# A graph attention layer on one core: the copy of a group's sums goes behind the next group's carried row, and the last two quads are weighted as one row of groups

## The chip, the cores and the metric

The kernel runs on one core of a Trainium2 chip. The core has five engines with instruction queues of their own: TensorE (PE, with its weight loads listed as PEld), VectorE (DVE), ScalarE (ACT), GpSimd (POOL) and SyncE (SP), which here issues the plain transfers. Each queue is worked off in order. The metric is the device time of one execution in microseconds, as the median over several runs. Times of single instructions come from one execution taken by the hardware profiler.

## The reference

12,500 nodes with 128 features each are joined by 200,000 edges, sorted by destination. Cut to what matters:

```python
h   = relu(layernorm(x));  hn = (h @ W_node.T).reshape(N, 4, 32)
e   = (edge_attr @ W_edge.T).reshape(E, 4, 32)
att = sum(concat([hn[src], hn[dst], e], -1) * a, -1);  att = where(att > 0, att, 0.2 * att)
m   = maximum(segment_max(att, dst), 0);  ex = exp(att - m[dst])
denom = segment_sum(ex, dst) + (E - deg)[:, None] * exp(-m)
out = x + segment_sum((ex / denom[dst])[..., None] * hn[src], dst)
```

So each destination needs the largest logit of its edges, a weighted sum of the gathered source rows, the sum of the weights and the number of its edges.

## The kernel before, in words

**Tiling.** The edges are cut into 392 groups of 511 (four chunks of 128, with one place left over), and four groups make a quad: 98 quads. Since the edges are sorted, a group's destinations lie in a window of 80 consecutive nodes. Quads are collected into supers of two to four quads (`supers`); the twenty in the middle have four. The logits of a super are brought into one softmax (`softmax`), while the groups of earlier quads are summed.

**Node stage.** At first the node rows are normalised and multiplied by the weights, and a table with 137 numbers a node is written to memory: the four heads' 32 values with a one each, a count and four logit parts.

**Gathers.** `gather` (L141) fetches 128 rows of the table for one chunk by an indirect transfer that POOL issues: 1494 from the table and 72 from `x` before the table is there. They run through a ring of eight quads, `ga`, and POOL issues them one behind the other.

**Logits.** `all_logits(q)` starts with `flush`, whose `add_sources` (L580) adds the source parts out of the gathered rows of the quad before it: it is the first instruction of a quad that needs that quad's gathers. Then, group by group, DVE compares destinations (L550) and PE multiplies (L556, L559).

**Sums.** `sums(q)` is a generator with one step for each group. A step weights the gathered rows (`weigh`, L766, 128x528 elements), makes the matrix that marks each edge's window place (L779), multiplies chunks 1 to 3 (L784), and then calls `complete()` for the group before it. The first place of chunk 0 is reserved for the *carried row*: row 96 of the sums of the group before that, scaled by DVE (L709) and with its count copied by ACT (L713), so that a destination whose edges run over a group's end is summed on. Then PE multiplies chunk 0 (L714), and ACT copies the 97x137 sums from PSUM to `pt` (L715). Three PSUM buffers named `acc` take the groups in turn. L709 and L715 of neighbouring groups read the same buffer, and DVE's instruction waits for ACT's.

**Division.** When a quad's last group is copied, ACT computes the exponentials of the denominator (L722), and `state["division"]` is left for the next `complete()`, where `divide` runs on DVE: L798, L801, L803, L807 (80x512), and L811, which adds `xw` to `res` (80x512; both in SBUF). SP then writes a row of windows for each group (L504), one in each step, each after the one before it because windows overlap. The last three quads are divided in parts, and three of the additions L811 are on POOL.

**Order.** All is under a manual schedule. `together` takes one step of each of its generators in turn: `sums` of one quad beside `all_logits` of another beside the stages of `softmax`. In the last super the flag is read that selects the slow path `tile_any_order`; it isn't taken for sorted edges.

**The two last quads.** For `q >= nq - 2` the window marks were made earlier on POOL (L741), and `weigh` runs one group ahead within its quad.

Of the kernel before, what the change touches and what calls it, by code (L numbers as in the profile page):

```python
# [16 lines left out]
H, HD = 4, 32  # L17
HW = HD + 1
# [6 lines left out]
R_CNT, R_SRC, ROW = H * HW, H * HW + 1, H * HW + 5  # L25
# [6 lines left out]
QG = 4  # L32
# [11 lines left out]
def blocks(total, step):  # L44
    return [(i, min(step, total - i)) for i in range(0, total, step)]
# [3 lines left out]
def kernel(  # L49
# [35 lines left out]
    nc = tc.nc  # L85
    NP = x.shape[0]
    G = dst_rows.shape[0]
# [34 lines left out]
    quads = blocks(G, QG)  # L122
    nq = len(quads)
# [6 lines left out]
    GA, GATHERED = {}, set()  # L130
# [26 lines left out]
    with tc.manual_schedule():  # L157
# [6 lines left out]
        for _ in range(AT_ONCE):  # L164
            q, i = early.pop(0)
# [301 lines left out]
    with tc.tile_pool(name="work", bufs=2) as work, \  # L467
# [13 lines left out]
        def groups(s):  # L481
            q0, m = supers[s]
            g0 = quads[q0][0]
            return g0, quads[q0 + m - 1][0] + quads[q0 + m - 1][1] - g0
# [30 lines left out]
        def fetch_inputs(q):  # L515
            g0, m = quads[q]
            xw = XW[q] = work.tile([SPAN, QG, D], F32, name="xw", bufs=4)
            at = ROWS[q] = windows(base_row, 4 * D, g0, m)
            due["inputs"] += [(as_bytes(xw[:, i, :]), rows_at(x, at[i], 4 * D)) for i in range(m)]
# [173 lines left out]
        begun = []  # L693
        state = {}

        def complete():

            division = None if "held" in state else state.pop("division", None)
            if begun:
                complete_group(*begun.pop())  # L700
            if division:
                divide(*division)

        def complete_group(q, i, ga, hot, pt, acc, fc):
            g0, m = quads[q]
            g = g0 + i
            if g:
                before = state["before"]
                nc.vector.tensor_tensor(  # L709
                    ga[0:1, i, 0, 0:H * HW].rearrange("p (h w) -> p h w", w=HW),  # L710
                    before[WIN:WIN + 1, 0:H * HW].rearrange("p (h w) -> p h w", w=HW),
                    fc.unsqueeze(2).to_broadcast([1, H, HW]), op=OP.mult)
                nc.scalar.copy(ga[0:1, i, 0, R_CNT:R_CNT + 1], before[WIN:WIN + 1, R_CNT:R_CNT + 1])  # L713
            nc.tensor.matmul(acc, hot[:, i, 0, :], ga[:, i, 0, :], start=False, stop=True)  # L714
            nc.scalar.copy(pt[:, i, :], acc)  # L715
            state["before"] = acc

            parts = {nq - 1: (2, 3), nq - 2: (2,), nq - 3: (2,)}.get(q, ())
            if i + 1 in parts or i == m - 1:
                lo = max([k for k in parts if k <= i], default=0)  # L720
                den = work.tile([SPAN, QG, H], F32, name="den")
                nc.scalar.activation(den[:, lo:i + 1, :], pt[0:SPAN, lo:i + 1, R_SRC:R_SRC + H],  # L722
                                     AF.Exp, scale=-1.0)
                state["division"] = q, pt, den, lo, i + 1


# [18 lines left out]
        def sums(q):  # L745

            for k in range(nq - 3, nq) if q == nq - 3 else [q] if q < nq - 3 else []:
                fetch_inputs(k)
            g0, m = quads[q]
            s = of_quad[q]  # L750
            s0, sm = groups(s)
            ga = GA.pop(q)
            heads = lambda t: t[:, :, 0:sm * H].rearrange("p j (h g) -> p j h g", h=H)
            ex, xs, facs = XS[s]
            fc = facs[WIN:WIN + 1, 0:sm * H].rearrange("p (h g) -> p h g", h=H)
            pt = work.tile([WIN + 1, QG, ROW], F32, name="pt", bufs=3)
            hot = HOT.pop(q) if q in HOT else marks(q)
            beside = xs[:, :, 0:sm * (H + 1)].rearrange("p j (h g) -> p g j h", g=sm)
            nc.scalar.copy(ga[:, :m, :, R_CNT:R_SRC + H], beside[:, g0 - s0:g0 - s0 + m])  # L759

            def weigh(i):

                if i < m:
                    val = ga[:, i, :, 0:H * HW].rearrange("p j (h w) -> p j h w", w=HW)
                    weight = heads(ex)[:, :, :, g0 + i - s0]
                    nc.vector.tensor_tensor(  # L766
                        val, val, weight.unsqueeze(3).to_broadcast([P, J, H, HW]), op=OP.mult)

            ahead = 1 if q >= nq - 2 else 0
            for i in range(ahead):  # L770
                weigh(i)
            for i in range(m):
                g = g0 + i
                if q == nq - 1 - FREE and i == 1:
                    for k in range(FREE):
                        HOT[nq - FREE + k] = marks(nq - FREE + k)
                weigh(i + ahead)
                if q < nq - FREE:
                    nc.vector.tensor_tensor(  # L779
                        hot[:, i, :, 0:SPAN], lane_ps.unsqueeze(1).to_broadcast([P, J, SPAN]),  # L780
                        slot[:, g, :].unsqueeze(2).to_broadcast([P, J, SPAN]), op=OP.is_equal)
                acc = ps.tile([P, 512], F32, name="acc", bufs=3)[0:WIN + 1, 0:ROW]
                for j in range(1, J):
                    nc.tensor.matmul(acc, hot[:, i, j, :], ga[:, i, j, :], start=j == 1, stop=False)  # L784
                complete()
                begun.append((q, i, ga, hot, pt, acc, fc[:, :, g - s0]))
                issue("inputs", "results", *(["inputs"] * 3 if q == nq - 3 else []))
                yield
# [90 lines left out]
        with tc.manual_schedule():  # L879
            for q in range(min(2, nq)):  # L880
                fetch(q)
                issue("weights", all_of=True)
            on_vector = nc.vector.tensor_copy
            assert supers[0] == (0, 2) and supers[1] == (2, 2)

            held = [(q, i) for q in range(raw, min(QUADS, nq)) for i in range(raws(q), quads[q][1])]
            GATHERED.update(range(raw, QUADS))

            def some(*numbers):
                for n in numbers:  # L890
                    for _ in range(min(n, len(held))):
                        held_gather(*held.pop(0), table, ROW)
                    yield

            together(some(2, 0, 1, 0, 1), *late(0, on_vector), normed(1))
            together(some(1, 0, 1, 0, 1), *late(1, on_vector), all_logits(0), normed(2))
            together(some(0, 0, 1), all_logits(1), raw_statistics(raw_pool, 3))
            check_steps = checked()
            for s, (q0, m) in enumerate(supers):


                ahead = list(range(q0 + m, sum(supers[s + 1]))) if s + 1 < len(supers) else []
                now, ahead = ahead[:1], ahead[1:]
                beside = [sums(q0 - 1)] if s not in (0, 2) else [] if s else late(2) + [raw_scaled(3)]
                beside += late(raw) if s == 1 else []
                turned_stage = softmax(s)
                if s == len(supers) - 1:

                    next(turned_stage)
                    redo = nc.values_load(flag[0:1, 0:1], min_val=0, max_val=1)  # L910
                    for _ in range(2):
                        next(beside[0])
                    state["held"] = True
                if not s:
                    beside.insert(0, some(1, 1, 1, 1, 1, len(held)))
                if s == len(supers) - 1:
                    together(turned_stage, *beside)
                else:
                    together(*beside, *map(all_logits, now), turned_stage)
                assert not held  # L920
                for k in range(m if s == 1 else m - 1):
                    now, ahead = ahead[:1], ahead[1:]
                    together(sums(q0 + k), *map(all_logits, now), *([] if s else [normed(raw)]))
                    if s > 4:
                        next(check_steps, None)
                if s == len(supers) - 2:
                    together(check_steps)
                if s < 2:
                    complete()
                for a in ahead:  # L930
                    together(all_logits(a))
                if not s:
                    together(*late(3))
            flush()
            last_sums = sums(nq - 1)
            together(last_sums)
            complete()
            complete()

    with tc.If(redo > 0):  # L940
# [195 lines left out]
```

## Time and profile before

| what | value |
|---|---|
| median of 3 runs | 2013.75 us (2011.76 to 2014.98) |
| the profiled execution: time, span | 2018.52 us, 2016.7 us |
| POOL busy | 1510.6 us, 75% of the span |
| DVE busy | 1323.2 us, 66% |
| PE busy | 1369.1 us, 68% |
| ACT busy | 406.3 us, 20% |
| mean granted TensorE clock | 0.539 |
| last gather issued | 1973.11 us to 1974.06 us |
| last DVE instruction ends | 2010.45 us |

A line of a group reads: source line, engine, operation, output and inputs with their shapes, count; then busy time and the mean of one in ns; then the idle time of the engine before them and what ended it. In the timeline a line reads: start and duration in us, engine, line, operation; the bracket is idle time before it and what ended it. In the list of waits: who waited for whom, the total in us, how often, the longest. POOL's busy share is below 100% because the time between two issues isn't counted as busy.

### The profile page before, as it was taken

The numbers are of one execution on the slowest core, as the hardware profiler recorded it, in microseconds if no ns is written. First come the engines' busy times: TensorE is split into PE (matmuls) and PEld (weight loads), VectorE is DVE, ScalarE is ACT, GpSimd is POOL, SyncE is SP. The second block draws the span as 40 slices with busy tenths as digits, with TensorE's granted clock in tenths as the row PEclk, the third lists the DMA queues.
The fourth block names the chain that finished last, engine by engine and source line by source line (L and its number), as shares of the span: only waits on it lengthen the run. The fifth ranks groups of instructions, "written<-read, shape, count | busy, mean of one in ns | idle before, by whom it ended". The sixth has DMA issues, their size and how long they took to land. (4 is left out here: it accounts for less than half of the span.)

```text
span 2016.7 us, 27090 instructions
## 1 busy us (share of the span) xinstructions
PE 1369.1 (68%) x7317; PEld 1243.8 (62%) x7317; DVE 1323.2 (66%) x3261; ACT 406.3 (20%) x1531; POOL 1510.6 (75%) x1609
## 2 busy tenths in 40 slices
PE   6577888766575757666757666666566666777776
PEld 5567788755565746555656566566565565766665
DVE  6676788666574766655656657556566475668776
ACT  6664122111111111111111111111111111112112
POOL 7777777777777777777777777777777777777774
PEclk8777555555555555555555555555555555555556
DMA  7654756544546455455545454545454545454531
GB/s 251 204 145 118 183 162 178 137 129 130 142 122 156 121 146 138 130 131 136 138 130 147 119 146 123 147 120 147 121 145 120 147 122 144 126 146 125 139 96 36
DMA packets 194091, 279.50 MB, mean 139 GB/s; under 512 B 79849, under 2 KB 143337, under 8 KB 186098
## 3 DMA queue, kind: packets, MB, share of 16 engines
q1 hardware_dynamic: 142128, 165.55, 30.0%
q0 software_dynamic: 50112, 109.61, 21.7%
q10 hardware_dynamic: 1698, 2.58, 0.4%
q8 instruction: 61, 1.00, 0.2%
q14 instruction: 92, 0.75, 0.1%
HBM read 254.25 MB, written 23.30 MB: 138 GB/s over the span
## 5 line engine op out<-in xcount | busy, mean ns | idle before, releaser
L141 POOL DMA_INDIRECT ga<-table,srci x1494 | 1422.9, 952 | 457.7 <-issue 384.0
L784 PE MATMUL acc<-ga,hot 128*97 128x137 f32 x2352 | 645.3, 446 | 54.1 <-ACT ga L759 25.4
L784 PEld LDWEIGHTS acc<-ga,hot 128*97 128x97 f32 x2352 | 516.8, 278 | 70.1 <-ACT ga L759 31.4
L556 PEld LDWEIGHTS <-at 80*128 80x128 bf16 x1568 | 211.0, 163 | 521.7 <-DVE at L550 504.4
L556 PE MATMUL lg<-pw,at 80*128 80x12 bf16 x1568 | 169.1, 181 | 445.8 <-DVE at L550 445.1
L559 PE MATMUL lg<-wblk,ea 128*128 128x8 f32 x1568 | 405.0, 356 | 0.0
L559 PEld LDWEIGHTS lg<-wblk,ea 128*128 128x128 f32 x1568 | 377.4, 306 | 0.0
L580 DVE TENSOR_TENSOR U<-st,ga 128x64 f32<-128x64 f32 x98 | 26.2, 268 | 436.1 <-DMA ga<-table,srci 428.8
L550 DVE TENSOR_TENSOR at<-const_ps,db 80x512 bf16<-80x512 f32 x392 | 267.3, 682 | 6.1
L766 DVE TENSOR_TENSOR ga<-ga,ex_ps 128x528 f32<-128x528 f32 x392 | 268.5, 685 | 0.6 <-issue 0.3
L714 PE MATMUL acc<-ga,hot 128*97 128x137 f32 x784 | 257.4, 431 | 2.8 <-ACT ga L713 2.7
L715 ACT COPY pt<-acc 97x137 f32<-97x137 f32 x392 | 107.4, 274 | 717.5 <-PE acc L714 715.1
L714 PEld LDWEIGHTS acc<-ga,hot 128*97 128x97 f32 x784 | 198.3, 282 | 4.9 <-ACT ga L713 4.6
L709 DVE TENSOR_TENSOR ga<-acc,facs 1x132 f32<-1x132 f32 x391 | 115.8, 296 | 121.8 <-ACT pt L715 111.9
L779 DVE TENSOR_TENSOR hot<-const_ps,slot 128x320 f32<-128x320 f32 x384 | 183.5, 478 | 0.0
L713 ACT COPY ga<-acc 1x1 f32<-1x1 f32 x391 | 59.9, 153 | 459.7 <-DVE ga L709 453.1
L141 POOL DMA_INDIRECT ga<-in_x_dram,srci x72 | 68.8, 955 | 23.1 <-issue 18.6
L807 DVE TENSOR_TENSOR res<-pt,const_ps 80x512 f32<-80x512 f32 (+2 forms) x102 | 67.5, 662 | 3.8 <-DVE const_ps L803 0.3
L811 DVE TENSOR_TENSOR res<-res,xw 80x512 f32<-80x512 f32 (+2 forms) x99 | 67.4, 681 | 3.4
L618 ACT ACTIVATE low<-t_ps 64x511 f32<-64x511 f32 (+2 forms) x28 | 16.5, 589 | 190.5 <-PE t_ps L616 190.5
L398 PE MATMUL row_ps<-wcat,hT 128*128 128x137 f32 x198 | 40.8, 358 | 20.7 <-DVE tgt L404 10.7
L568 DVE TENSOR_REDUCE st<-lg 128x64 f32<-128x192 f32 x98 | 35.0, 357 | 25.5 <-PE lg L559 24.6
(137 smaller groups left out, 1012.8 us busy)
## 6 DMA issues: line engine op xcount, KB each, us to landing
db<-in_dst_dram SPq DMA_DIRECT2D x98, 640.0 KB
ea<-in_edge_t_dram SPq DMA_DIRECT2D x98, 512.0 KB
ga<-table,srci POOLq DMA_INDIRECT x1494
xw<-in_x_dram SPq DMA_DIRECT2D x392, 40.0 KB
out_dram<-res SPq DMA_DIRECT2D x392, 40.0 KB
pw<-side SPq DMA_DIRECT2D x392, 1.9 KB
table<-row SPq DMA_DIRECT2D x9, 616.5 KB
xt<-in_x_dram SPq DMA_DIRECT2D x9, 576.0 KB
```

Of the source, the lines that this page charges most:

```text
L141: nc.gpsimd.indirect_dma_start(out=ga[:, i, j, 0:width], out_offset=None, in_=rows, in_offset=bass.IndirectOffsetOnAxis(ap=srci[:, g0 + i, ...
L550: nc.vector.tensor_tensor(at[:, i, :], node_ps[0:SPAN, g0 + i:g0 + i + 1].to_broadcast([SPAN, GE]), db[:, i, :], op=OP.is_equal)
L556: nc.tensor.matmul(lg[:, i, j].rearrange("p k h -> p (k h)"), at[:, i, j * P:(j + 1) * P], sw, start=i + j == 0, stop=False, skip_group_ch ...
L559: nc.tensor.matmul(lg[:, i, 2 * w:2 * w + 2, 0, :], ea[:, i, w, :], wblk, start=False, stop=True, skip_group_check=True)
L709: nc.vector.tensor_tensor(ga[0:1, i, 0, 0:H * HW].rearrange("p (h w) -> p h w", w=HW), before[WIN:WIN + 1, 0:H * HW].rearrange("p (h w) -> ...
L714: nc.tensor.matmul(acc, hot[:, i, 0, :], ga[:, i, 0, :], start=False, stop=True)
L715: nc.scalar.copy(pt[:, i, :], acc)
L766: nc.vector.tensor_tensor(val, val, weight.unsqueeze(3).to_broadcast([P, J, H, HW]), op=OP.mult)
L779: nc.vector.tensor_tensor(hot[:, i, :, 0:SPAN], lane_ps.unsqueeze(1).to_broadcast([P, J, SPAN]), slot[:, g, :].unsqueeze(2).to_broadcast([ ...
L784: nc.tensor.matmul(acc, hot[:, i, j, :], ga[:, i, j, :], start=j == 1, stop=False)
L807: nc.vector.tensor_tensor(res[:, :n, :].rearrange("p g (h d) -> p g h d", d=HD), val[:, :, :, 0:HD], share_ps[0:R, :n, :].unsqueeze(3).to_ ...
L811: add.tensor_tensor(res[:, :n, :], res[:, :n, :], xw, op=OP.add)
```

## The change

Four things are changed. `complete_group` is cut into `carry` (the carried row, and then the copy of the group *before*), `finish` (the last multiplication) and `copy_out` (copy, exponentials, leaving the division). So the copy of a group's sums stands on ACT behind the next group's L709 and L713 rather than ahead of them; since the division is left by the copy, it comes one step later. In the last two quads, a step calls `carry()` first, and weights a group ahead only then, and the two quads are one row: the last quad's first group is weighted in the last step of the quad before. Their two copies L759 are both made before that. A pending division is done at once where the last super begins, and the ends get another `complete()` and a `copy_out()`. The number of instructions of each kind is unchanged.

```diff
             if begun:
-                complete_group(*begun.pop())
+                carry()
+                finish(*begun.pop())
             if division:
                 divide(*division)
-        def complete_group(q, i, ga, hot, pt, acc, fc):
+        def carry():
+            if not begun or "carried" in state:
+                return
+            q, i, ga, hot, pt, acc, fc = begun[0]
+            state["carried"] = True
+            if quads[q][0] + i:
                 before = state["before"]
                 nc.vector.tensor_tensor(
...
                 nc.scalar.copy(ga[0:1, i, 0, R_CNT:R_CNT + 1], before[WIN:WIN + 1, R_CNT:R_CNT + 1])
+            copy_out()
+
+        def finish(q, i, ga, hot, pt, acc, fc):
+            del state["carried"]
             nc.tensor.matmul(acc, hot[:, i, 0, :], ga[:, i, 0, :], start=False, stop=True)
+            state["before"] = acc
+            state["uncopied"] = q, i, pt, acc
+
+        def copy_out():
+            if "uncopied" not in state:
+                return
+            q, i, pt, acc = state.pop("uncopied")
+            m = quads[q][1]
             nc.scalar.copy(pt[:, i, :], acc)
-            state["before"] = acc
...
-            ahead = 1 if q >= nq - 2 else 0
-            for i in range(ahead):
-                weigh(i)
+            if q == nq - 2:
+                weigh(g0)
             for i in range(m):
...
-                weigh(i + ahead)
+                if last_two:
+                    carry()
+                weigh(g + last_two)
...
+                    divide(*state.pop("division"))
                     state["held"] = True
...
                 if s < 2:
                     complete()
+                    copy_out()
...
             together(last_sums)
             complete()
+            complete()
+            copy_out()
             complete()
```

More of the change, by code (lines that the diff above doesn't have):

```diff
@@ L699, in complete @@
             if begun:
-                complete_group(*begun.pop())
+                carry()
+                finish(*begun.pop())
             if division:
                 divide(*division)
-        def complete_group(q, i, ga, hot, pt, acc, fc):
-            g0, m = quads[q]
-            g = g0 + i
-            if g:
+        def carry():
[4 more added lines that the diff above has]
+            if quads[q][0] + i:
                 before = state["before"]
@@ L723, in complete_group @@
                                      AF.Exp, scale=-1.0)
+                assert "division" not in state
                 state["division"] = q, pt, den, lo, i + 1
@@ L751, in sums @@
             s0, sm = groups(s)
-            ga = GA.pop(q)
+            ga = GA[q]
             heads = lambda t: t[:, :, 0:sm * H].rearrange("p j (h g) -> p j h g", h=H)
@@ L758, in sums, with weigh @@
             beside = xs[:, :, 0:sm * (H + 1)].rearrange("p j (h g) -> p g j h", g=sm)
[L759 to L765, printed above, removed]
+            last_two = q >= nq - 2
+            for k in (nq - 2, nq - 1) if q == nq - 2 else () if last_two else (q,):
+                lo, n = quads[k][0] - s0, quads[k][1]
+                nc.scalar.copy(GA[k][:, :n, :, R_CNT:R_SRC + H], beside[:, lo:lo + n])
+            def weigh(g):
+                k = g // QG
+                if g < G and (k == q or last_two):
+                    val = GA[k][:, g - k * QG, :, 0:H * HW].rearrange("p j (h w) -> p j h w", w=HW)
+                    weight = heads(ex)[:, :, :, g - s0]
                     nc.vector.tensor_tensor(
                         val, val, weight.unsqueeze(3).to_broadcast([P, J, H, HW]), op=OP.mult)
-            ahead = 1 if q >= nq - 2 else 0
-            for i in range(ahead):
-                weigh(i)
+            if q == nq - 2:
+                weigh(g0)
             for i in range(m):
```

## The prediction

> **What bounds the kernel now.** I read the page's groups first, then the list of waits, and then the timeline at one quad and at the end.
>
> ```profile
> L141 POOL DMA_INDIRECT ga<-table,srci x1494 | 1422.9, 952 | 457.7 <-issue 384.0
> L580 DVE TENSOR_TENSOR U<-st,ga 128x64 f32<-128x64 f32 x98 | 26.2, 268 | 436.1 <-DMA ga<-table,srci 428.8
> L709 DVE TENSOR_TENSOR ga<-acc,facs 1x132 f32<-1x132 f32 x391 | 115.8, 296 | 121.8 <-ACT pt L715 111.9
> ...
> L811 DVE TENSOR_TENSOR res<-res,xw 80x512 f32<-80x512 f32 (+2 forms) x99 | 67.4, 681 | 3.4
> ```
>
> ```profile
> POOL ga L141 <- issue: 402.6, 1320, 0.3
> ...
> DVE U L580 <- DMA ga<-table,srci: 428.8, 75, 11.9
> ...
> DVE ga L709 <- ACT pt L715: 111.9, 153, 2.2
> ```
>
> POOL issues a gather every 1.25 us (0.95 and 0.30) from the start to 1974.06 and, once the table is there, is never kept longer than 0.3. DVE waits for its rows at L580, 428.8 us in all. So POOL sets the pace up to 1974, and the 111.9 us that L709 waits for the copy lie, but for the last ones, inside DVE's larger wait. Shortening them is worth nothing there; only the end behind the last gather, or the length of a gather, can move the time.
>
> Gathers are not all equally long. The timeline, at a common quad and at another:
>
> ```profile
> 1011.81 0.95 POOL L141 DMA_INDIRECT ga<-table,srci  x1 [0.31 <-issue]
> 1011.93 0.27 DVE L580 TENSOR_TENSOR U<-st,ga 128x64 f32<-128x64 f32 x1 [5.68 <-DMA ga<-table,srci]
> ...
> 1013.79 0.30 DVE L709 TENSOR_TENSOR ga<-acc,facs 1x132 f32<-1x132 f32 x1
> ...
> 1015.57 0.94 POOL L141 DMA_INDIRECT ga<-table,srci  x1 [0.30 <-PE acc L784]
> 1015.58 0.71 DVE L811 TENSOR_TENSOR res<-res,xw 80x512 f32<-80x512 f32 x1
> 1016.00 0.28 ACT L715 COPY pt<-acc 97x137 f32<-97x137 f32 x1 [1.72 <-PE acc L714]
> ```
>
> ```profile
> 1336.28 0.69 DVE L811 TENSOR_TENSOR res<-res,xw 80x512 f32<-80x512 f32 x1
> 1336.37 1.42 POOL L141 DMA_INDIRECT ga<-table,srci  x1 [0.30 <-PE acc L784]
> ```
>
> Here L811 began 0.09 before the gather, and the gather took 1.42. Write d for L811's start less the gather's: d of -0.21 gave 1.30 (at 1763.02), -0.27 gave 1.24 (1158.26), -0.46 gave 1.05 (1078.10); d from 0.00 up gave 0.94 to 0.95. All fit one rule of this trace: the gather needs something at 0.13 us after its start, and waits until an L811 already running has ended: stretch = 0.56 + d, for d between -0.56 and about -0.03. L606, the only other long one of that kind, does the same (1.45 at 1374.35, d -0.04). Of the 10.6 us of stretch in this execution, 4.5 us fall on L811 (15 gathers) and 4.5 us on L606 (12). In the common quad L811 begins just as the gather does, and costs nothing.
>
> **The change part by part.**
>
> *Copy behind the carry, gathers still running.* ACT's L715 no longer stands before L709; per group DVE loses a wait of about 0.48 and ACT gets one. Worth nothing by itself: DVE waits at L580 for 5.7 to 8 us a quad. If that cover were gone it would be a gain, so it is costed at 0. PSUM buffers: a copy ends about 0.3 us behind L713, while L714 behind the same L713 takes 0.66, so PE finds its buffer free: 0.
>
> *The division moved by one step.* This moves L811 against the gathers' clock. Take the quad above. L709 at 13.79 stays. The next step now follows at once: L550 at +0.33, L766 +0.61, L779 +0.61, end of DVE's part +0.50, so 1015.84. L709 then waits for PE: L714 is done when ACT's copy began, 1016.00. L709 to L811 took 1.76 in unhindered quads (1315.04 to 1316.80). So L811 begins at 1017.77, and the gathers on the old clock at 1018.07 (1015.57 and two times 1.25): d = -0.30, stretch 0.26. This repeats: in 40 quads from 370 us on the copy stands 4.07 us behind L580, and L580 stands a fixed landing time behind a gather (mostly 0.05 to 0.16). Setting L811 at 4.07 + 1.76 behind each of these 40 L580s gives d from -0.57 to 0.50, most at -0.26 to -0.35, and stretches that add to 8.7 us. A stretched gather shifts all later ones and with them the next L580, so they add up.
>
> In quads with L606 (at 1293) the division's 2.04 no longer stand behind the first L709; L621 loses 0.15 of that to ACT's L618, so the second L709 comes at 1299.05 in place of 1300.94, L811 at 1300.81, the gather at 1301.34: d = -0.53, 0.03 each, for the 22 of them from 370 us on 0.7 us. In the 18 quads behind a softmax the same working gives 0.1 us. The old 4.5 us of L811 go; L606 keeps its place behind L580 and its 4.5. Net: 8.7 + 0.7 + 0.1 - 4.5 = +5.0 us. The unknown is d. If all 40 places are 0.15 earlier, the 40 cost 4.2; 0.2 later, 14.0; 0.3 later, 7.2 and falling. That makes the net between +0.5 and +10.3.
>
> The Trainium skill, GPSIMD Engine Reference, Key points, says that GpSimd shares its SBUF interfaces with VectorE, with contention from instructions with two SBUF inputs, and names no moment. By that alone L580 (0.12 behind a gather's start) or an L811 anywhere over a gather would cost too, before as after, and the change nothing; the trace has 0.94 to 0.95 us for these gathers, so the row decides.
>
> *SP's queue.* The output rows wait for L811 and so does what stands behind them: `pw`, `xw`, `ea` and `db` up to 2.2 us later. `pw` and `ea` are fetched two quads (40 us) ahead, `db` and `xw` about one (20 us): 0. POOL's queue keeps its order.
>
> *The end.* At the last super's start the division now stands behind carry, count, copy and exponential: L709 at 1974.19, then 0.30, 0.15, 0.28, 0.22 and 0.03 between each: L798 at 1975.23 in place of 1974.82, +0.41, and L580, L616 and the chain behind them. One division earlier leaves the way for L568, which waited for PE until 1970.18: PE then finds L550 0.75 sooner and loses 0.4 again a group later, -0.33. In the last two quads a link was L714, copy, L709, L713, L714: 1.36 (1997.33 to 1998.69); without the copy 1.05. But DVE fills it: by group 0.33 for L709, 0.61 for L766 and half of a division's 1.0, 1.45. Placing the rows in the new order, both L759 first, I get the first division of the last quad done at 2006.8 - 0.33 = 2006.5 in place of 2007.61. Behind it stand the four last output rows, 2007.64, 2009.14, 2011.87 and 2013.48: each waits for the one before, 1.5 to 2.7 us, so the end is theirs. Rows of the quads before hold some of it back: -0.6, between -1.3 (all of it) and +0.4 (nothing of the 0.33, and one more row of 2.7).
>
> Sum: +5.0 - 0.6 = +4.4 us. The profiled execution took 2018.52 (its span 2016.7 and 1.8 around it); it would take 2022.9. The median of the runs shown is 4.8 lower: 2013.75 + 4.4 = 2018.2.
>
> **The rivals.**
>
> *B, L811 misses the gathers.* If the second L709 begins 0.30 later, as it did before behind the copy, d is about 0.0 and no gather is stretched. Then only the old 4.5 us vanish: 2013.75 - 4.5 - 0.6 = 2008.7. It decides from 0.26 us later on. For it: landing times without the profiler aren't seen. Against: the copy's 4.07 is the same within 0.02 in nearly every such quad.
>
> *C, the gathers pay the same in all.* More L606 or L811 stretches without the profiler before, or fewer after, so that the sums cancel: the end alone, 2013.2. For it: 10 of the 40 L580s stand 0.3 to 1.2 behind a gather, so the landings do slip. The skill's rule taken without a moment gives this time too.
>
> *D, the end turns slower.* The granted clock in the last stage was 1.00 from 1995 to 2001, and 0.50 from 2002 to 2005. At 0.50 L784 repeats after 1.90 (1972.04 to 1973.94), longer than DVE's 1.45; with all at 0.50 the first division of the last quad comes 2.1 later: with the gathers as in C, 2015.3. The skill's TensorE: Matmul & The Clock Gate, part 1, grants full clock behind about 3.4 us of work; the 0.99 at 1988 to 1990, behind 3.8 us of unused multiplications, agrees.
>
> **How the numbers follow.** About 0.2%, 4.0 us, is what a measurement can tell from no change here. Forecast 0.66, of which 0.56 above 4.0 and 0.10 below (its d earlier by 0.1 or more); B 0.10, of which 0.07 faster and 0.03 within; C 0.18, within; D 0.06, of which 0.05 within and 0.01 above, on top of some stretch. Faster 0.07, within 0.36, slower 0.57. The range: up to +12.2 (the +10.3, +0.4 from the end and 1.5 for D), 2026; down to 2011, between B and C, which leaves out B and the forecast's far end. The forecast's own is 2013.7 (+0.5 - 0.6) to 2023.5 (+10.3 - 0.6).
>
> **What would show it.** Right: gathers of 1.15 to 1.3 us about once in each common quad, with an L811 begun 0.2 to 0.4 before them; L141's mean 4 to 6 ns higher; the last gather 5 us later against the first; L709 behind PE, never ACT; first division of the last quad about 1 us nearer to the last gather. Wrong: L811 at d above 0 or below -0.56 in the common quads, or stretched gathers without an L811; or an L709 that still waits 0.3 longer.

## The result, and the profile after

The changed kernel takes **2023.53 us** (median of 6 runs, 2020.85 to 2026.14), the kernel before 2014.37 (6 runs, 2011.76 to 2016.00). The ratio is 1.0044, with a 95% interval from 1.0033 to 1.0055: slower by 6.6 to 11.1 us, where 2018.2 us (+4.4) was forecast, with a range from 2011 to 2026. The kernel is slower, as forecast, but the 9.2 us between the medians are about twice the +4.4. The profiled execution of the changed kernel took 2026.14 us; its span is 2024.4, against 2016.7 before.

The groups of the changed kernel that answer to those shown of before (L713 was L709, L833 was L811), from the page:

```profile
L141 POOL DMA_INDIRECT ga<-table,srci x1494 | 1431.3, 958 | 457.8 <-issue 396.3
L580 DVE TENSOR_TENSOR U<-st,ga 128x64 f32<-128x64 f32 x98 | 26.4, 270 | 483.9 <-DMA ga<-table,srci 476.7
...
L713 DVE TENSOR_TENSOR ga<-acc,facs 1x132 f32<-1x132 f32 x391 | 115.8, 296 | 59.4 <-PE acc L722 51.4
```

And the list of waits of the changed kernel (who waits for whom: us in total, times, longest):

```profile
DVE U L580 <- DMA ga<-table,srci: 476.7, 79, 12.7
...
POOL ga L141 <- issue: 415.5, 1363, 0.3
...
DVE ga L713 <- PE acc L722: 51.4, 137, 2.3
```

The change did what it says. The carried row waited 111.9 us for ACT's copy; now it waits 51.4 us, and for PE. Nothing came of these 60 us: DVE's wait at L580 grew from 428.8 to 476.7 us. POOL, once the table is there, is still never kept longer than 0.3 us, so it still sets the pace. What grew is the gathers themselves, from 952 to 958 ns in the mean. The last one starts at 1981.60 us instead of 1973.11.

A common quad of the changed kernel, from the timeline (start, duration, engine, line):

```profile
1323.22 0.94 POOL L141 DMA_INDIRECT ga<-table,srci  x1 [0.31 <-issue]
1323.55 0.27 DVE L580 TENSOR_TENSOR U<-st,ga 128x64 f32<-128x64 f32 x1 [2.84 <-DMA ga<-table,srci]
...
1325.42 0.29 DVE L713 TENSOR_TENSOR ga<-acc,facs 1x132 f32<-1x132 f32 x1
...
1327.64 0.30 DVE L713 TENSOR_TENSOR ga<-acc,facs 1x132 f32<-1x132 f32 x1 [0.19 <-PE acc L722]
1327.96 0.17 DVE L820 SCALAR_TENSOR_TENSOR den<-pt,den 80x16 f32<-80x16 f32 x1
...
1329.40 0.69 DVE L833 TENSOR_TENSOR res<-res,xw 80x512 f32<-80x512 f32 x1
1329.49 1.41 POOL L141 DMA_INDIRECT ga<-table,srci  x1 [0.30 <-PE acc L806]
```

Read it downwards: L580 begins 0.33 behind a gather's start, the division starts behind the second L713 (before, behind the first), and so L833 begins 0.09 ahead of a gather, which then takes 1.41 us instead of 0.94. In this execution 52 gathers are stretched in this way.

The next table sums it up for every execution profiled. "Stretch" is what all 1566 gathers took above 0.947 us (in brackets, at the addition and at L606, how many took 0.98 or more); "end" is the span less the last gather's start. The experiments follow below.

| kernel | stretch at the addition | at L606 | all | last gather starts | end | span |
|---|---|---|---|---|---|---|
| before | 4.5 (15) | 4.5 (13) | 10.6 | 1973.11 | 43.6 | 2016.7 |
| before, second profile | 3.8 (13) | 3.8 (12) | 9.1 | 1970.06 | 43.3 | 2013.4 |
| changed | 13.9 (52) | 3.5 (12) | 19.9 | 1981.60 | 42.8 | 2024.4 |
| changed, second profile | 11.8 (46) | 2.9 (11) | 17.6 | 1978.61 | 43.0 | 2021.6 |
| changed, product in PSUM | 1.0 (9) | 2.5 (11) | 5.9 | 1964.86 | 44.2 | 2009.1 |
| before, product in PSUM | 3.0 (7) | 2.2 (9) | 6.6 | 1964.30 | 45.6 | 2009.9 |
| changed, useless work everywhere | 18.9 (56) | 5.7 (18) | 27.7 | 1984.85 | 44.2 | 2029.0 |
| changed, useless work in 40 quads | 2.6 (32) | 4.0 (16) | 9.5 | 1967.02 | 43.8 | 2010.8 |
| changed, division at the old step | 8.1 (35) | 3.7 (12) | 14.6 | 1973.17 | 45.5 | 2018.7 |
| changed, old order at the end | 13.1 (54) | 5.7 (16) | 21.5 | 1978.48 | 44.1 | 2022.6 |
| changed, product and L606 by PSUM | 1.5 (6) | 0 | 4.8 | 1965.26 | 44.7 | 2010.0 |

Span less stretch less end is 1957 to 1963 us in all of them, while the stretch runs from 5 to 28. The two pairs of before and after agree: +9.3 and +8.5 us of stretch, -0.8 and -0.3 at the end, and spans longer by 7.7 and 8.2. (The remaining 5 us are mostly the unstretched gather's own interval, 1.248 us in some executions and 1.251 in others; why was not found.)

### The profile page after: what moved, and what is told of

Its sections match the earlier page's. It is cut to its first block, busy times and chain, and to the rows that moved or that the text cites. A ratio compares the mean times of both kernels' runs of the same rounds, so it can differ in the third digit from the quotient of the medians.

```text
span 2024.4 us, 26960 instructions
## 1 busy us (share of the span) xinstructions
PE 1365.6 (67%) x7317; PEld 1241.2 (61%) x7317; DVE 1325.0 (65%) x3261; ACT 405.3 (20%) x1531; POOL 1518.5 (75%) x1609
## 4 chain that ended last, share of the span: by engine, by line
POOL 23%; PE 22%; DVE 18%; issue 16%; DMA 13%; ACT 3%; SPq 0%; DVEq 0%; ACTq 0%; POOLq 0%
POOL ga L141 23%; DMA ga<-table,srci 12%; PE acc L806 9%; PE lg L559 6%; DVE at L550 3%; PE acc L722 2%; DVE res L829 2%; DVE res L833 2%; PE lg L556 1%; DVE run L625 1%; DVE ga L713 1%; DVE ga L787 1%; PE t_ps L616 1%; PE acc L280 1%; DVE t_ps L652 1%
## 5 line engine op out<-in xcount | busy, mean ns | idle before, releaser
L806 PE MATMUL acc<-ga,hot 128*97 128x137 f32 x2352 | 633.6, 440 | 66.2 <-issue 25.3
L806 PEld LDWEIGHTS acc<-ga,hot 128*97 128x97 f32 x2352 | 510.1, 275 | 83.0 <-ACT ga L779 29.2
L580 DVE TENSOR_TENSOR U<-st,ga 128x64 f32<-128x64 f32 x98 | 26.4, 270 | 483.9 <-DMA ga<-table,srci 476.7
L722 PE MATMUL acc<-ga,hot 128*97 128x137 f32 x784 | 254.6, 427 | 3.1 <-ACT ga L717 3.0
L722 PEld LDWEIGHTS acc<-ga,hot 128*97 128x97 f32 x784 | 196.5, 279 | 4.3 <-ACT ga L717 3.9
L713 DVE TENSOR_TENSOR ga<-acc,facs 1x132 f32<-1x132 f32 x391 | 115.8, 296 | 59.4 <-PE acc L722 51.4
L829 DVE TENSOR_TENSOR res<-pt,const_ps 80x512 f32<-80x512 f32 (+2 forms) x102 | 67.5, 662 | 3.6
L833 DVE TENSOR_TENSOR res<-res,xw 80x512 f32<-80x512 f32 (+2 forms) x99 | 66.9, 676 | 3.4
L672 PE MATMUL ex_ps<-ident,ex 64*128 64x64 f32 (+2 forms) x112 | 18.2, 310 | 58.0 <-ACT ex L659 58.0
```

Of the source, the lines that this page charges most:

```text
L713: nc.vector.tensor_tensor(ga[0:1, i, 0, 0:H * HW].rearrange("p (h w) -> p h w", w=HW), before[WIN:WIN + 1, 0:H * HW].rearrange("p (h w) -> ...
L829: nc.vector.tensor_tensor(res[:, :n, :].rearrange("p g (h d) -> p g h d", d=HD), val[:, :, :, 0:HD], share_ps[0:R, :n, :].unsqueeze(3).to_ ...
L833: add.tensor_tensor(res[:, :n, :], res[:, :n, :], xw, op=OP.add)
```

## The experiments

In what follows, d is the addition's start less the gather's, and a common quad is one whose addition stands outside the softmax stages: nearly always one of the first two of a super of four. Theory: a DVE instruction with both inputs in SBUF that already runs at 0.13 us after a gather's start holds the gather until it ends, and the change moves L833 to just that place. Rivals: any long DVE instruction does so; the copy's new place or the later output rows are what costs; the time is DVE's own; the order at the end costs.

**1. The same instructions at the same places, but the addition reads one input from PSUM.** Outside the softmax stages the division's product goes to the idle bank of `t_ps` (`turning` is set while a softmax holds it):

```diff
+            part = res
+            if q < nq - 3 and "turning" not in state:
+                part = ps.tile([P, GE], F32, name="t_ps")[0:R, 0:n * D].rearrange("p (g d) -> p g d", d=D)
             nc.vector.tensor_tensor(
-                res[:, :n, :].rearrange("p g (h d) -> p g h d", d=HD), val[:, :, :, 0:HD],
+                part[:, :n, :].rearrange("p g (h d) -> p g h d", d=HD), val[:, :, :, 0:HD],
                 share_ps[0:R, :n, :].unsqueeze(3).to_broadcast([R, n, H, HD]), op=OP.mult)
-            add.tensor_tensor(res[:, :n, :], res[:, :n, :], xw, op=OP.add)
+            add.tensor_tensor(res[:, :n, :], part[:, :n, :], xw, op=OP.add)
```

> The changed kernel, but outside the softmax stages the division's product is left in PSUM, so that the addition has one input in SBUF and one in PSUM instead of two in SBUF; order and count of instructions as in the changed kernel. Theory (a running addition with both inputs in SBUF holds the gather 0.13 us after its start): of the 13.85 us by which L833 stretched gathers in the changed kernel at least 11 go, though the additions stand where they stood; some stay in softmax stages; about 2023.5 - 12 = 2011.5 us, L141's mean back from 958 to about 950 ns. Rival 1 (any long DVE instruction there, whatever its inputs): no change, 2023.5 us. Rival 2 (the new copy order or the later output rows cost the time, and the stretches are hidden): stretches go, the time stays within 3 us of 2023.5.

Measured: **2012.28 us**, beside 2013.27 for the kernel before (ratio 0.9989, 0.9980 to 0.9998). The whole loss is gone. The timeline of this version at two quads, the first with the product in PSUM (L838 reads `t_ps`), the second in a softmax stage, where it stayed in SBUF (L838 reads `res`):

```profile
775.24 0.69 DVE L835 TENSOR_TENSOR t_ps<-pt,const_ps 80x512 f32<-80x512 f32 x1
...
775.96 0.69 DVE L838 TENSOR_TENSOR res<-t_ps,xw 80x512 f32<-80x512 f32 x1
776.05 0.94 POOL L141 DMA_INDIRECT ga<-table,srci  x1 [0.30 <-issue]
...
1758.84 0.69 DVE L838 TENSOR_TENSOR res<-res,xw 80x512 f32<-80x512 f32 x1
1759.04 1.30 POOL L141 DMA_INDIRECT ga<-table,srci  x1 [0.30 <-issue]
```

The first begins 0.09 before the gather, as in the quad above that cost 0.47, lasts 0.69 as there, and the gather takes 0.94. In this execution 31 additions from PSUM begin 0.05 to 0.50 before a gather, and all 31 gathers take 0.94 or 0.95; the second, from SBUF, begins 0.20 before one, and it takes 1.30. So it is the two inputs in SBUF that count and not the place or the length, and the stretch is what the change costs. The Trainium skill, SBUF — State Buffer, Who interferes with whom, says that a DVE instruction with at most one SBUF input, outside its two-port modes, does not contend with GpSimd; these 31 rows agree.

**2. The kernel before with its product in PSUM** (the same edit).

> The kernel before with the same product in PSUM. Theory: only the 4.5 us of L811's stretches can go, so about 2014.4 - 4 = 2010.4 us, and the distance to the changed kernel with its product in PSUM shrinks from 9.2 us to that of the end and of other stretches, under 2 us. Rival 1: 2014.4 us. Rival 2: the distance stays near 9 us, whatever both gain.

Measured: 2012.31 us (ratio 0.9995, 0.9986 to 1.0004). The distance to the changed kernel with the same edit is 0.03 us (each median within about 2) where it was 9.2: with the addition out of the gathers' way, copy, division and the two last quads' new order together change nothing that the times show. The kernel's own gain is 1 us, which the interval does not tell from none, and not the expected 4. Not all of L811's stretches could go: in the profile seven additions that stayed in SBUF for a softmax still stretch gathers by 3.0 us. In all it has 6.6 us of stretch against 9.1 and 10.6 before, and its end is 2 us longer (45.6); so some of the gain is given back at the end, by an execution's phases or by the edit, which was not separated.

**3. Useless work ahead of the product.** Two reciprocals into a scratch tile in each division:

```diff
             nc.vector.reciprocal(share_ps[0:R, :n, :], den)
+            if q < nq - 3:
+                idle = work.tile([SPAN, QG, H], F32, name="idle", bufs=1)
+                for _ in range(2):
+                    nc.vector.reciprocal(idle[:, :n, :], den)
```

> The changed kernel with two useless reciprocals of 80x16 numbers (0.26 to 0.29 us each) in every division ahead of the product, so that the addition stands 0.5 to 0.58 us later; DVE works about 50 us more in all. Theory: shifting every addition of the changed kernel's trace by that and adding up the rule's stretches gives 6 to 7 us where it was 13.9, so about 2016.5 us: more work, less time. Rival 1 (the time is DVE's, or lies in what waits for the division): 2023.5 us or more, up to 2030 if a tenth of the added work shows.

Measured: **2029.75 us** (ratio 1.0079, 1.0065 to 1.0093), so the expectation failed, and by its number a rival has it. The trace says where. The two reciprocals took 0.47 together and moved the addition by 0.39, not by 0.5 to 0.58. In most common quads d is now +0.10 to +0.60, and nothing is stretched there, as expected. But in the 40 quads at and behind a softmax (the last two of each super of four), 32 now stand at d of -0.08 to -0.32, most at about -0.12. In the changed kernel's first profile 15 of them stood at about -0.51 and paid 0.05 each, and the shift by 0.39 puts those there; 18 stood above 0, and why most of these came there too, by other landings, stays open. One of the 40, from this version's timeline (L837 is the addition):

```profile
417.27 0.68 DVE L833 TENSOR_TENSOR res<-pt,const_ps 80x512 f32<-80x512 f32 x1
417.99 0.69 DVE L837 TENSOR_TENSOR res<-res,xw 80x512 f32<-80x512 f32 x1
418.10 1.39 POOL L141 DMA_INDIRECT ga<-table,srci  x1 [0.30 <-issue]
```

These quads make 14.1 of the addition's 18.9 us. If that reading is right, the same work in the common quads alone must make the kernel faster.

**4. The same useless work in 40 divisions alone**, the first two of each super of four.

```diff
-            if q < nq - 3:
+            q0, quads_in = supers[of_quad[q]]
+            if quads_in == 4 and q - q0 < 2:
```

> The changed kernel with the two useless reciprocals in the 40 divisions alone whose additions stand in common quads (the first two of each super of four); in the run with the reciprocals everywhere they moved an addition by 0.39 us. Theory: the common quads' d goes from -0.38 to -0.09 to 0.0 to 0.3, where nothing is stretched, and the other additions keep their -0.5 at 0.05 each; L833's 12 to 14 us fall to 1 to 3, so 2011 to 2014 us with 15 us more of DVE work, and the loss of the run with reciprocals everywhere lies in the quads at and behind a softmax, moved from d of -0.51 to -0.12. Rival (what the useless work costs there is DVE's time, and the gathers' stretch is not what is paid for): 2023.5 to 2030 us.

On the chip of this run the kernel before took 2535.5 us too, and this one 2537.5, with DVE and PE waiting for stretches of 10 us in which ACT did nothing that the trace shows. It says nothing on the question, and the kernel was run again:

> The same kernel again, since on the chip of that run the kernel before took 2535.5 us as well, with ACT standing still for 10 us at a time. The changed kernel with two useless reciprocals in the first two divisions of each super of four. Theory: the common quads' additions move by 0.39 us to d of 0.0 to 0.3, L833's 12 to 14 us of stretches fall to 1 to 3, 2011 to 2014 us, with 15 us more of DVE work. Rival (the time is DVE's): 2023.5 to 2030 us.

Measured: **2015.75 us** (ratio to the kernel before 1.0016, 1.0007 to 1.0025): 7.8 us less than the changed kernel's 2023.5 (2.3 above the kernel before beside it, where the changed kernel stands 9.2 above), with 40 times 0.47 us more work on DVE. The addition in a common quad of this version (L838):

```profile
473.73 0.68 DVE L834 TENSOR_TENSOR res<-pt,const_ps 80x512 f32<-80x512 f32 x1
474.32 0.94 POOL L141 DMA_INDIRECT ga<-table,srci  x1 [0.30 <-issue]
474.45 0.69 DVE L838 TENSOR_TENSOR res<-res,xw 80x512 f32<-80x512 f32 x1
```

It begins 0.13 after the gather and costs it nothing. The addition's stretches add to 2.6 us where the changed kernel has 13.9 and 11.8, within the expected 1 to 3; the time missed the expected 2011 to 2014 by 2 us. The rival (DVE's own time, 2023.5 to 2030) is out.

**5. The division at its old step**, the copy still behind the carried row, so that the division waits for copy and exponentials:

```diff
-            division = None if "held" in state else state.pop("division", None)
             if begun:
                 carry()
                 finish(*begun.pop())
+            division = None if "held" in state else state.pop("division", None)
```

> The changed kernel with the division taken in the same step in which the copy leaves it, as early as before the change; the copy stays behind the carried row, so the division waits for copy and exponentials. By the trace L833 then begins 2.50 us behind L713 and 4.37 behind L580, in common quads at d of -0.53 (landing as in the kernel before, 0.1 behind a gather) to -0.38 (0.25 behind one, as in the changed kernel). Theory: stretches of 0.03 to 0.18 in 40 quads, 1 to 7 us in all where it was 13.9: 2011 to 2017 us. Rival (the copy order itself costs the 9 us): 2022 to 2025 us.

Measured: 2021.03 us (ratio 1.0045, 1.0031 to 1.0059), above the expected 2011 to 2017. L833 stands 4.36 behind L580 as worked out, but the landings did not keep their place: L580 begins 0.01 to 1.16 behind a gather's start, so that the common quads spread over all d, and the quads behind a softmax, which the expectation left out, came to d of -0.24 to -0.37 in seven of the twenty supers of four. That is 8.1 us at the addition in place of 1 to 7. The end is 45.5 us, 2.5 to 2.7 more than in the changed kernel; that the division's wait for ACT (92.2 us in all, 96 times) has no cover there is the likely reason, and was not tried. This run alone would not tell the theory from its rival; runs 1 and 2 do.

**6. Both kernels once more, unchanged, for second profiles.**

> The kernel before, unchanged, for a second profiled execution. If the phases are a property of the kernel, L580 stands 0.05 to 0.16 us behind a gather in most common quads again, L811 stretches gathers by 4 to 5 us and all stretches add to about 10.6 us. If they change from execution to execution, these sums move by several us although the kernel is the same, and the first profile was one draw. Time: the kernel before's, 2013 to 2014 us.

> The changed kernel, unchanged, for a second profiled execution beside that of the kernel before. If the landing that stood 0.1 to 0.15 us later than in the kernel before belongs to the change, L580 stands 0.16 to 0.33 behind a gather again and L833 stretches by 13 to 14 us; if it belongs to the execution, L833's sum lies anywhere between 8 (landings as in the first profile of before) and 14 us. Time: 2021 to 2024 us.

Measured: 2014.18 and 2023.45 us. In the 36 common quads from 365 to 1900 us, L580 begins behind a gather's start by (median) 0.12 in the first profile of before and 0.19 in the second, and by 0.25 and 0.23 in the changed kernel. So part of this place changes from one execution to the next, and 0.04 to 0.13 remains between the kernels in these two pairs. The stretches at L833 in these quads add to 10.2 and 9.1 us, and in all to 13.9 and 11.8: the second lies between what was expected for a place that belongs to the change (13 to 14) and the first landings of before (8).

**7. The old order in the last two quads** (weights within each quad, carried row behind the weighting, one copy for each quad):

```diff
-            for k in (nq - 2, nq - 1) if q == nq - 2 else () if last_two else (q,):
+            for k in (q,):
...
-                if g < G and (k == q or last_two):
+                if k == q and g - g0 < m:
...
-            if q == nq - 2:
+            if last_two:
                 weigh(g0)
...
-                if last_two:
-                    carry()
```

> The changed kernel with the last two quads weighted as before the change (each quad for itself, carried row behind the weighting, each quad's own copy of the weights). By the prediction's step on the end 0.3 us come back at the first division of the last quad and up to 1.3 at the end: 2023.5 + 0.6 = 2024.1 us, gathers unchanged. Rival (the order of the last two quads is what costs): 2014 to 2018 us.

Measured: 2023.08 us (ratio 1.0050, 1.0036 to 1.0064); the changed kernel beside it 2023.45. The times can't tell them apart. In the profile the end takes 44.1 us against 42.8 and 43.0, as expected, and that is all this says. The rival, that the order of the last two quads is what costs, is out.

**8. L606 out of the gathers' way as well.** ACT copies the destinations to PSUM (0.58 us each), and L606 compares SBUF with PSUM, on top of the edit of run 1:

```diff
-            nc.vector.tensor_tensor(kp[:R, 1:GE], dr[:R, 1:NE + 1], dr[:R, 0:NE], op=OP.is_equal)
+            state["turning"] = True
+            t_ps = ps.tile([P, GE], F32, name="t_ps")
+            nc.scalar.copy(t_ps[:R, 0:NE], dr[:R, 0:NE])
+            nc.vector.tensor_tensor(kp[:R, 1:GE], dr[:R, 1:NE + 1], t_ps[:R, 0:NE], op=OP.is_equal)
```

> The changed kernel with the product in PSUM as before, and the other long instruction with two inputs in SBUF changed too: ACT copies the 64x511 destinations to PSUM, and L606 compares SBUF with PSUM. Theory: of the 5.9 us of stretches that the version with the product in PSUM still had, the 2.5 us at L606 go, so 2.5 us below that version, 2009.8 us. Rival 1 (a compare at L606 is on DVE's path behind the landing and its input doesn't matter): as that version, 2012.3 us, or more by the added 0.7 us copies of ACT in 22 quads.

Measured: **2010.97 us** (ratio 0.9988, 0.9979 to 0.9997). L606 stretches nothing any more; the seven that begin 0.29 to 0.47 before a gather leave it at 0.94. The time lies between the expected 2009.8 and the rival's 2012.3 and does not decide; these gathers do. The group of the gathers in this version, from its page:

```profile
L141 POOL DMA_INDIRECT ga<-table,srci x1494 | 1413.5, 946 | 459.0 <-issue 387.9
```

Its mean is 946 ns, against 958 in the changed kernel. The gain on run 1 is 1.3 us by the medians, which the intervals don't separate. It is the fastest of the kernels tried, and faster than the kernel before by 0.6 to 4.2 us.

## Why the prediction was right, and where its size was off

**POOL sets the pace, and L709's shorter wait is worth nothing.** Right: 60 us less of that wait, 48 us more at L580, and with the stretches taken away the change is worth 0.03 us (runs 1 and 2).

**The rule, 0.56 + d.** Right, and within 0.013 us for each of the 52 gathers that L833 stretched in the changed kernel (in its second profile for 49, three of them by under 0.03). Its cause was argued from two lines alike; run 1 shows it. Had it been "any long DVE instruction", L829 (one input in PSUM), which begins 0.72 ahead of L833, would have stretched those gathers that L833 follows by 0.2 to 0.6; there are 27 of them, at 0.94 to 0.96. The Trainium skill's sentence in GPSIMD Engine Reference, Key points, taken without a moment, would have had the change cost nothing there; the moment decides.

**L833's place, d of about -0.30.** This is the term that was mis-sized. L833 stands 5.85 behind L580 (worked out: 5.83), but L580 does not stand where it stood: 0.25 behind a gather's start in place of 0.12. So d is mostly -0.09 to -0.25, nearer to the costliest place, and 36 common quads cost 10.2 us, where 40 had been taken at 8.7. The prediction took one execution's landings as the kernel's; a second profile of the same kernel moved them by 0.07. Why they stand later still in the changed kernel was not found. The prediction had priced such a shift ("0.2 later, 14.0") and kept it for the range.

**The other quads.** In quads with L606 the addition stands 8.28 behind L580 as worked out (8.27), but the landings spread: eight of 23 came to d of -0.51 to -0.53, at 0.03 to 0.06 each, and nearly all others lie above 0 and cost nothing. All quads outside the common ones and after 365 us cost 2.2 in place of 0.8, and 1.5 us fell before 365 us, where the prediction counted nothing. Together: 13.9 in place of 9.5. L606 did not keep its 4.5: it fell by 1.0 in the first pair and by 0.9 in the second.

**The net.** +9.3 us of stretch (second pair +8.5) where +5.0 was taken, within the bound of +10.3. The 13.9 in place of 9.5 and L606's 1.0 less make +3.4 of the 4.3 between; the rest lies at gathers beside neither.

**The end, -0.6.** In the first pair -0.8, in the second -0.3. The first division of the last quad ends 33.72 us behind the last gather's start, 34.50 before: -0.78, where -1.1 was worked out. L580 of the last super comes 0.93 later against the last gather, not 0.41. These lines carry it, of the kernel before and then of the changed kernel:

```profile
1973.11 0.95 POOL L141 DMA_INDIRECT ga<-table,srci  x1 [0.30 <-issue]
...
1974.82 0.17 DVE L798 SCALAR_TENSOR_TENSOR den<-pt,den 80x16 f32<-80x16 f32 x1
...
1977.04 0.26 DVE L580 TENSOR_TENSOR U<-st,ga 128x64 f32<-128x64 f32 x1
...
2007.19 0.42 DVE L811 TENSOR_TENSOR res<-res,xw 80x256 f32<-80x256 f32 x1
```

```profile
1981.60 0.94 POOL L141 DMA_INDIRECT ga<-table,srci  x1 [0.30 <-issue]
...
1983.93 0.24 DVE L820 SCALAR_TENSOR_TENSOR den<-pt,den 80x16 f32<-80x16 f32 x1 [0.82 <-ACT den L738]
...
1986.46 0.25 DVE L580 TENSOR_TENSOR U<-st,ga 128x64 f32<-128x64 f32 x1
...
2014.90 0.42 DVE L833 TENSOR_TENSOR res<-res,xw 80x256 f32<-80x256 f32 x1
```

The division held here waits 0.82 for ACT's exponentials, as the prediction's added chain says, and it takes longer itself: 2.53 us from its first instruction to L580, 2.22 before. In both it runs beside POOL's window marks, which can lengthen it (last section); how much of the 0.31 is theirs was not separated.

**The rivals.** B (no stretch at all, 2008.7) did not come: 27 of the 36 common quads stand in the window, at a median d of -0.18. C (the sums cancel, 2013.2) fell with the two pairs of profiles. D is not seen: the end is shorter, not longer.

## What to carry to other kernels

Where POOL issues indirect transfers back to back and is the bound, an instruction of another engine can set the time without being on any wait: read the duration of single issues, not their mean, and put the long ones beside what DVE is running. Then change the operands rather than the schedule, because a place between two clocks is a draw that the next edit, or the next execution, draws again: leaving one input in PSUM brought both kernels to 2012.3 us, while shifting the same instruction by 0.39 us gave -8 or +6 us depending on which quads were shifted. Delays of the phase kind are to be forecast as a range over the phase, with a second profile where one can be had.

## What the runs showed of the hardware that was not expected

- **One DVE instruction stretches a gather even when it comes second.** L833 (80 partitions) or L606 (64) begun 0.0 to 0.6 after a gather's start cost it nothing. L886, part of the test for sorted edges, compares two inputs in SBUF on 128 partitions, and begun 0.16 to 0.53 after a gather's start it stretched all of the eight seen in eleven executions: the gather then ended 1.49 to 1.50 behind L886's start. Its last block, with 8 partitions, cost nothing at +0.08 to +0.24. In the changed kernel:

```profile
624.35 1.70 POOL L141 DMA_INDIRECT ga<-table,srci  x1 [0.30 <-issue]
...
624.55 0.68 DVE L886 TENSOR_TENSOR low<-rows 128x511 f32<-128x511 int32 x1
```

So the number of partitions matters for this instruction, but it is not all: L580, both inputs in SBUF on 128 partitions but only 0.27 long, began 0.0 to 0.6 behind a gather's start some 700 times in these executions, and none of those gathers took over 0.99. What makes the difference was not tried. The prediction took L606 for the only other long instruction of the kind; this one (L864 before the change) is another, with 0.6 of the 10.6 us of stretch.
- **A gather does not hold the DVE instruction, but another POOL instruction does.** The 80x512 addition took 0.69 to 0.73 us whether it ran across a gather's start or began 0.13 behind it. Once in each execution it runs beside POOL's window marks (L758, before the change L741; 0.47 us each in the median). With both inputs in SBUF it then took 0.78 to 1.06 us in nine executions, and one of the marks beside it 0.89 to 1.17. With one input in PSUM, as in runs 1 and 2, it took 0.69, and the mark that ran wholly within its time 0.47. The changed kernel's line, and that of run 1:

```profile
1985.69 0.84 DVE L833 TENSOR_TENSOR res<-res,xw 80x512 f32<-80x512 f32 x1
```

```profile
1969.42 0.69 DVE L838 TENSOR_TENSOR res<-t_ps,xw 80x512 f32<-80x512 f32 x1
```

- **The place of a landing against the gathers' clock is partly a property of the execution**: 0.12 and 0.19 us for the same kernel, in the median over 36 quads.
